# Layer 0 of a four-layer graph network: adjacency tiles transposed by the DMA engines, codes made in place, a fifth accumulator

## The chip, the core and the metric

The kernel runs on one core of a Trainium2 chip. A core has five engines that run side by side, each with its own queue of instructions: TensorE (PE, matmuls and transposes; PEld is its loading of weights), VectorE (DVE), ScalarE (ACT), GpSimd (POOL) and SyncE (SP, which here only issues DMAs). Sixteen DMA engines move data between HBM and the on-chip memory SBUF. TensorE writes its results to PSUM, a memory of eight banks.

The metric is the device time of one launch in microseconds (us). The trace comes from a separate execution with the hardware profiler on; its own time stands beside its span in the table below.

## The reference

Four graph layers follow each other on a node matrix x (4096 x 256, float32) and one adjacency matrix adj (4096 x 4096, int32, about 0.8% ones). Each layer adds its result to x. Layer 0 is the one that the change touches, and of it the attention:

```python
h = relu(layernorm(x))
Wh = h @ W
e = Wh @ a_src + (Wh @ a_dst).T
e = where(e > 0, e, 0.2 * e)
e = where(adj > 0, e, -9e15)
h_attn = softmax(e, axis=1) @ Wh
...   # dense branches on Wh, gating with h_attn, layernorm; x = x + result
```

Layer 1 averages neighbours (adj == 1), layer 2 is a second attention of the same kind (slope 0.01), layer 3 a dot-product attention masked by adj. All of them need adj with its columns on the partitions, that is transposed, since the matmul `acc += y.T @ v` sums over the columns of adj.

## The kernel before

**Codes.** An adjacency tile of 128 rows x 1024 columns is a unit. There are 128 units: g runs over 8 blocks b of 512 rows, 4 quarters q of the columns and 4 row tiles r in a block. Units are turned once, in layer 0, and changed into two-valued bf16 codes (a very large number where adj is 0, a very small one where it is 1): ACT computes exp(scale * adj + bias) with scale and bias of fixed logarithms. Four units (r = 0 to 3) fill one tile `turned[b, q]` (128 x 4 x 8 x 128 bf16, 1 MB). SP stores every such tile to HBM (`codesT`, L368), from where layers 1, 2 and 3 load it.

**How a unit is turned (`fresh(g)`, L345 to L361).** POOL issues the load, which also casts int32 to bf16 (L351, eight buffers `adj_t`). PE makes eight 128x128 transposes with the bf16 identity `identb` into one PSUM bank `cT` (L354, a pool with a single buffer, L343). ACT reads that bank and writes the codes to SBUF (L358).

**Preparation.** `block0(b)` (L378), for eight row blocks staggered by two ticks: three units made fresh, the load of x (L382, on SP), layernorm on DVE, POOL and ACT (L133), transposes, projection with W (L201 to L214), and then `reach`, below.

**Attention (`run`, L271).** A block has 16 pairs of column tiles, 128 pairs in all. Iteration n of the loop does, in program order: `ahead(n)`, which makes unit n + 24 fresh (`UPB` = 16, `FRESH` = 8) and at every fourth n issues the store; `reach(n + 19)`, two DVE steps (L229) of a running minimum over the columns, from which the next block's row maxima come; `logits`, two DVE instructions (L265) and one on POOL that subtracts the codes (L269); and for the pair three iterations earlier (`lag`) two exponentials on ACT (L295) and eight matmuls (L306, each issued as two 128x257 passes) into four accumulators, one for each row tile. At the end of a block, reciprocals of the sums (L314) and `finish0`, which scales the accumulators into `xs` by turns on ACT (L336) and DVE (L334).

**The maxima.** At a block's last `reach`, `run` is copied by ACT (L235), transposed by PE (L238), reduced by DVE, transposed again (L248), copied (L250), and sent through HBM by two small DMAs on SP (L251, L253). The result `ab_row` is needed by L263 (ACT), after which DVE can begin the logits of the next block.

**Order.** The program is written in one order, and a planner reorders the instructions of each engine by dependencies and its own estimate of their times; so the trace shows L265 and L229 in turn although each comes twice in a row in the program. What it decided is then fixed: each engine, SP among them, goes through its queue in order and waits at the first instruction that isn't ready. Buffers are pools with a number of slots; an instruction that needs a slot waits for the last reader of its previous tile.

**PSUM.** Eight banks: `run`, `top`, `b` one each, `cT` one, and four accumulators. Layer 2 runs the same class with five accumulators (L794), loading stored codes instead of making them.

## Time and profile before

| | |
|---|---|
| median of 3 runs | 3092.0 us (3091.15 to 3102.12) |
| the profiled execution | 3085.67 us, span 3083.9 us |
| layer 0's preparation | 0 to about 112 us |
| layer 0's attention | about 112 to 630 us |
| its blocks end (first L314 of each) | 178.9, 247.2, 313.7, 381.2, 447.3, 514.6, 573.1, 629.7 us |
| PE busy over the span | 2869.8 us, 93% |
| DVE, ACT, POOL busy | 1851.4, 1271.7, 873.3 us |
| L354, transposes of adjacency | 1024, 83.2 us busy on PE |
| L358, codes on ACT | 128, 141.5 us busy |
| L351, loads | 128 of 256 KB, 4.5 us from issue to landing |
| L368, stores of codes | 32 of 1 MB, 5.1 us |

Times in the trace count from the span's start. A row of a group of instructions gives the line, the engine, the operation, output and inputs, the number of instructions and their mean duration; PE's durations overlap, as matmuls are pipelined, so what one costs is read from the pitch between starts. A window's row gives start and end, length, then the busy time of PE, PEld, DVE, ACT and POOL with the number of instructions, the share of the clock that TensorE was granted, the mean busy share of the sixteen DMA engines and GB/s. The waits name an instruction, what ended its wait, the sum, the count and the longest. An arrow <- stands before what released an engine.

### The profile page before, as it was taken

The numbers are of one execution on the slowest core, as the hardware profiler recorded it, in microseconds if no ns is written. First come the engines' busy times: TensorE is split into PE (matmuls) and PEld (weight loads), VectorE is DVE, ScalarE is ACT, GpSimd is POOL, SyncE is SP. The second block draws the span as 40 slices with busy tenths as digits, with TensorE's granted clock in tenths as the row PEclk, the third lists the DMA queues.
The fourth block names the chain that finished last, engine by engine and source line by source line (L and its number), as shares of the span: only waits on it lengthen the run. The fifth ranks groups of instructions, "written<-read, shape, count | busy, mean of one in ns | idle before, by whom it ended". The sixth has DMA issues, their size and how long they took to land.

```text
span 3083.9 us, 34813 instructions
## 1 busy us (share of the span) xinstructions
PE 2869.8 (93%) x13344; PEld 2336.0 (76%) x13344; DVE 1851.4 (60%) x3306; ACT 1271.7 (41%) x1924; POOL 873.3 (28%) x605
## 2 busy tenths in 40 slices
PE   5799999979999999699977999999999999999999
PEld 4688888845555555588856888788888888888888
DVE  5767676324444444544479888755856656656653
ACT  5655655358888884400044443444211211211211
POOL 3556665532333233100016555661000000000000
PEclk9899999989999999899998999999999999999999
DMA  8666664054444341234322222202111111111100
GB/s 209 144 132 136 126 139 110 7 178 129 142 129 132 122 132 40 87 110 147 99 103 82 76 77 81 76 7 69 57 38 37 58 37 37 58 37 37 56 8 7
DMA packets 103127, 268.75 MB, mean 87 GB/s; under 512 B 10704, under 2 KB 24272, under 8 KB 94768
## 3 DMA queue, kind: packets, MB, share of 16 engines
q1 hardware_dynamic: 79104, 220.30, 21.4%
q0 software_dynamic: 22464, 45.51, 8.7%
q8 instruction: 104, 1.70, 0.2%
q10 hardware_dynamic: 1392, 0.72, 0.1%
q14 instruction: 63, 0.52, 0.1%
HBM read 262.22 MB, written 37.81 MB: 97 GB/s over the span
## 4 chain that ended last, share of the span: by engine, by line
PE 27%; issue 25%; DVE 3%; POOL 2%; DMA 1%; ACT 1%; POOLq 0%; DVEq 0%; ACTq 0%
PE acc L306 12%; PE acc L723 8%; PE s L150 3%; PE mm L150 2%; PE acc L960 2%; DVE run L229 1%; POOL y L269 1%; DMA turned<-codesT 1%; DVE y L265 1%; POOL pl_rs L116 1%; POOL out_dram L973 1%; DVE pl_st L121 0%; ACT y L295 0%; DVE hT L109 0%; PE tp L144 0%
## 5 line engine op out<-in xcount | busy, mean ns | idle before, releaser
L306 PE MATMUL acc<-v,y 128*128 128x257 f32 x4096 | 927.1, 385 | 42.5 <-ACT y L295 19.9
L306 PEld LDWEIGHTS acc<-v,y 128*128 128x128 f32 x4096 | 774.4, 192 | 158.1 <-ACT hp L754 22.7
L269 POOL TENSOR_TENSOR y<-y,turned 128x1024 f32<-128x1024 f32 x256 | 547.1, 2150 | 307.7 <-DVE y L265 267.5
L295 ACT ACTIVATE y<-y,sdst 128x512 f32<-128x512 f32 x512 | 342.9, 714 | 367.7 <-POOL y L269 367.5
L265 DVE SCALAR_TENSOR_TENSOR y<-ab_row,cdst,b 128x512 f32<-128x512 f32 x512 | 362.1, 743 | 180.2 <-PE acc L306 115.8
L960 PE MATMUL acc<-v,y 128*128 128x257 f32 x2048 | 454.5, 380 | 0.4 <-DVE rden L968 0.4
L150 PE MATMUL s<-qT,hT 128*128 128x256 f32 x2048 | 445.2, 379 | 0.7 <-ACT qT L908 0.7
L150 PEld LDWEIGHTS s<-qT,hT 128*128 128x128 f32 x2048 | 389.0, 190 | 54.2 <-ACT qT L908 1.4
L960 PEld LDWEIGHTS acc<-v,y 128*128 128x128 f32 x2048 | 387.1, 190 | 55.9 <-issue 0.8
L953 ACT ACTIVATE y<-y 128x1024 f32<-128x1024 f32 x128 | 132.2, 1055 | 714.3 <-DVE y L952 710.0
L229 DVE SCALAR_TENSOR_TENSOR run<-turned,sd,run 128x512 f32<-128x512 bf16 x496 | 373.4, 753 | 49.8 <-DMA turned<-codesT 28.3
L513 ACT ACTIVATE sign<-a,limits 128x1024 bf16<-128x1024 int32 x256 | 293.8, 1148 | 79.6 <-DMA a<-in_adj_dram 75.0
L973 POOL DMA_DIRECT2D out_dram<-o x32 | 17.4, 543 | 933.7 <-DVE rden L968 931.1
L723 PE MATMUL acc<-v,eq 128*128 128x512 f32 x1024 | 239.3, 395 | 0.1
L922 DVE SCALAR_TENSOR_TENSOR y<-code,s 128x512 f32<-128x512 bf16 x256 | 175.8, 687 | 100.5 <-PE s L150 100.2
L723 PEld LDWEIGHTS acc<-v,eq 128*128 128x128 f32 x1024 | 192.6, 188 | 44.9 <-DVE eq L719 0.3
L952 DVE TENSOR_TENSOR y<-y,top 128x1024 f32<-128x1024 f32 x128 | 146.2, 1216 | 43.0 <-PE top L946 43.0
L929 DVE TENSOR_TENSOR mx<-mx,y 128x512 f32<-128x512 f32 x224 | 154.8, 691 | 7.4
L358 ACT ACTIVATE turned<-cT,log_wide 128x1024 bf16<-128x1024 bf16 x128 | 141.5, 1106 | 33.5 <-PE cT L354 33.2
L719 DVE TENSOR_SCALAR eq<-code 128x4096 fp32r<-128x4096 bf16 x32 | 73.4, 2293 | 114.8 <-PE acc L723 114.8
L150 PE MATMUL mm<-hsT,w_L_gnn_W_hz 128*128 128x512 f32 x256 | 117.4, 598 | 0.6 <-DVE hsT L576 0.6
L354 PE MATMUL cT<-identb,adj_t 128*128 128x128 bf16 x1024 | 83.2, 226 | 36.4 <-DVE identb L67 18.5
(222 smaller groups left out, 2717.3 us busy)
## 6 DMA issues: line engine op xcount, KB each, us to landing
a<-in_adj_dram SPq DMA_DIRECT2D x128, 512.0 KB, 3.8
adj_t<-in_adj_dram POOLq DMA_DIRECT2D x128, 256.0 KB, 4.5
codesT<-turned SPq DMA_DIRECT2D x32, 1024.0 KB, 5.1
code<-codesT SPq DMA_DIRECT2D x128, 256.0 KB, 3.8
turned<-codesT SPq DMA_DIRECT2D x32, 1024.0 KB, 5.4
code<-codesT SPq DMA_DIRECT2D x64, 512.0 KB, 4.9
ab_row<-l_ab_d SPq DMA_DIRECT2D x16, 512.0 KB, 3.9
xs<-in_x_dram SPq DMA_DIRECT2D x8, 512.0 KB, 11.0
```

Source lines behind the costliest of these rows:

```text
L150: nc.tensor.matmul(out=ps, lhsT=lhsT_of(k), rhs=rhs_of(k), start=(k == 0), stop=(k == n - 1))
L229: nc.vector.scalar_tensor_tensor(st["run"], code, self.sd[:, j, 1:2], st["run"], ALU.subtract, ALU.min)
L265: nc.vector.scalar_tensor_tensor(y[:, :, k, :], st["ab"][:, 0, :, :], self.cdst[:, c + k : c + k + 1], st["b"], ALU.add, ALU.max,)
L269: nc.gpsimd.tensor_tensor(y, y, mask[:, :, c % QT : c % QT + 2, :], ALU.subtract)
L295: nc.scalar.activation(y[:, :, k, :], y[:, :, k, :], AF.Exp, bias=self.sdst[:, c + k : c + k + 1],)
L306: nc.tensor.matmul(out=accs[b][r], lhsT=y[:, r, k, :], rhs=self.v[:, c + k, :], start=(c + k == 0), stop=(c + k == NT - 1),)
L513: nc.scalar.activation(sign, a, AF.Sign, bias=limits[:, v : v + 1], accum_out=over[:, t, v, q : q + 1],)
L723: nc.tensor.matmul(out=acc, lhsT=eq[:, ts(c, P)], rhs=v1[:, c, :, :], start=(c == 0), stop=(c == NT - 1),)
L922: nc.vector.scalar_tensor_tensor(y[:, :, c : c + 2, :], st["code"][:, :, c : c + 2, :], -BIG / UNIT, ps, ALU.mult, ALU.add,)
L929: nc.vector.tensor_tensor(mx, mx, y[:, :, c : c + 2, :], ALU.max)
L952: nc.vector.tensor_tensor(part, part, top, ALU.subtract)
L960: nc.tensor.matmul(out=accs[r], lhsT=st["y"][:, r, c, :], rhs=v3[:, c, :], start=(c == 0), stop=(c == NT - 1),)
```

## The change

A unit is no longer transposed by PE. `fresh` is split in three steps that run at different leads. `load(g)` issues the load on POOL as before. `turn(g)` issues on SP one transposing DMA from the loaded tile to its quarter of `turned[b, q]`, SBUF to SBUF. ACT then computes the codes in place in `turned`. When unit g is made fresh, the load of unit g + 6 and the transposing DMA of unit g + 3 are issued just before its exponential; the first call issues six loads and three transposes ahead. The numbers of buffers stay at eight each. The identity in bf16 and the PSUM pool `cT` go, and the free bank becomes a fifth accumulator of layer 0's attention. Layers 1 to 3 and the dense part of layer 0 are as they were.

```diff
-    identb = const.tile([P, P], BF16, name="identb")
-    nc.vector.tensor_copy(identb, ident)
...
+    LOADED, TURNED = 6, 3
...
-            ps_c = es.enter_context(tc.tile_pool(name="ps_c", bufs=1, space=PSUM))
-
-            def fresh(g):
-
+            raw, units = {}, NRB * UPB
+
+            def load(g):
                 b, q, r = g // UPB, g % UPB // RB, g % RB
-                t = b * RB + r
-
-                a = adj_p.tile([P, QW], BF16, tag="adj", name="adj_t")
-                nc.gpsimd.dma_start(out=a, in_=adj[ts(t, P), ts(q, QW)])
-                ps = ps_c.tile([P, QW], BF16, tag="cT", name="cT")
-                for i in range(QT):
-                    nc.tensor.transpose(ps[:, ts(i, P)], a[:, ts(i, P)], identb)
+                raw[g] = adj_p.tile([P, QW], BF16, tag="adj", name="adj_t")
+                nc.gpsimd.dma_start(out=raw[g], in_=adj[ts(b * RB + r, P), ts(q, QW)])
+
+            def turn(g):
+                b, q, r = g // UPB, g % UPB // RB, g % RB
                 if r == 0:
                     turned[b, q] = turned_p.tile([P, RB, QT, P], BF16, tag="turned", name="turned")
-                ct = turned[b, q][:, r, :, :]
+                nc.sync.dma_start_transpose(turned[b, q][:, r, :, :], raw.pop(g))
+
+            def fresh(g):
+
+                if g == 0:
+                    for k in range(LOADED):
+                        load(k)
+                    for k in range(TURNED):
+                        turn(k)
+                if g + LOADED < units:
+                    load(g + LOADED)
+                if g + TURNED < units:
+                    turn(g + TURNED)
+                b, q, r = g // UPB, g % UPB // RB, g % RB
+                ct = turned[b, q][:, r, :, :].rearrange("p c i -> p (c i)")
                 nc.scalar.activation(
-                    ct.rearrange("p c i -> p (c i)"), ps, AF.Exp,
-                    scale=math.log(UNIT / WIDE), bias=log_wide,
+                    ct, ct, AF.Exp, scale=math.log(UNIT / WIDE), bias=log_wide
                 )
...
-            att.run(es, LEAD, 4, ahead)
+            att.run(es, LEAD, 5, ahead)
```

## The prediction, made before the changed kernel ran

> **What bounds the kernel now.** I read the page's busy shares first, then cut layer 0 by the reciprocals that close each block of rows (L314 starts at 178.89, 247.15, 313.66, 381.19, 447.31, 514.58, 573.15 and 629.75 us) and asked for the windows between them. The first matmul of the attention is at 114.9 us, so layer 0's attention runs from about 112 to 629.75: 517.7 us of 3083.9. All that the change touches lies there and in the 112 us ahead of it.
>
> Windows of the span, columns window, length, then busy us of PE, PEld, DVE, ACT, POOL, clock, DMA share, GB/s. The first two are preparation, the next three are blocks 0, 3 and 7 of layer 0's attention, the last two are blocks of layer 2's:
>
> ```profile
> 50.00:60.00 10.00, 8.40 (x65) 7.20 (x65) 5.79 (x16) 10.00 (x19) 3.19 (x5) 1.00 1.02 222
> 60.00:70.00 10.00, 9.45 (x81) 8.22 (x80) 7.16 (x21) 9.89 (x20) 2.54 (x5) 1.00 0.97 211
> ...
> 112.00:178.89 66.89, 62.49 (x336) 53.73 (x337) 50.98 (x81) 40.12 (x56) 51.06 (x32) 0.95 0.39 82
> 313.66:381.19 67.53, 64.79 (x390) 55.57 (x389) 46.39 (x76) 39.43 (x54) 42.63 (x33) 1.00 0.63 133
> 573.15:629.75 56.60, 55.78 (x257) 48.50 (x256) 14.01 (x25) 14.36 (x23) 20.71 (x10) 1.00 0.00 1
> ...
> 1813.32:1875.08 61.76, 58.24 (x261) 50.00 (x261) 49.14 (x78) 25.03 (x39) 34.86 (x17) 0.97 0.22 77
> 1996.69:2052.76 56.07, 54.89 (x254) 47.65 (x255) 32.73 (x53) 24.50 (x38) 33.55 (x17) 1.00 0.03 10
> ```
>
> The attention is bound by TensorE: 64.8 of 67.5 us, while DVE has 46.4, POOL 42.6, ACT 39.4. Block 7, which has no adjacency left to turn, takes 56.6. The preparation from 40 to 80 us is bound by ACT (10.0 of 10 us) with the DMA engines full beside it (share 1.02). The timeline inside block 3 shows what a pair costs on PE:
>
> ```profile
> 331.60 0.61 PE L354 MATMUL cT<-identb,adj_t 128*128 128x128 bf16 x8
> 332.05 3.69 PE L306 MATMUL acc<-v,y 128*128 128x257 f32 x16
> 335.57 0.61 PE L354 MATMUL cT<-identb,adj_t 128*128 128x128 bf16 x8
> 336.02 3.69 PE L306 MATMUL acc<-v,y 128*128 128x257 f32 x16
> ```
>
> A pair begins every 3.97 us (335.57 - 331.60). In block 7 the DVE's y (which waits for PE there) comes every 3.47 us (582.57, 586.04, 589.51), so eight transposes cost PE 0.50 us. The windows of L354 count 128 of them in each of blocks 1 to 5, 80 in block 0, 40 in block 6, none in block 7; 264 lie ahead of 112 us.
>
> ```profile
> q1 hardware_dynamic: 79104, 220.30, 21.4%
> q0 software_dynamic: 22464, 45.51, 8.7%
> ...
> adj_t<-in_adj_dram POOLq DMA_DIRECT2D x128, 256.0 KB, 4.5
> codesT<-turned SPq DMA_DIRECT2D x32, 1024.0 KB, 5.1
> ```
>
> These lines of the page price a unit (one 128x1024 adjacency tile) on the DMA engines. Between 80 and 112 us units came every 2.21 us (POOL issued at 97.51, 99.72, 101.94) at a share of about 1.04: 2.3 us of all sixteen engines for one load and a quarter of a store.
>
> **What the Trainium skill says.** (1) "Advanced Engine Details and Errata", X-Bar Transpose (TRN2): transposing DMAs are as fast as plain ones, 350 to 400 GB/s. (2) "DMA: Bandwidth & Descriptors", Latency and other measured facts: 261 GB/s effective with a non-contiguous middle dimension. A unit is 262,144 bytes, so these give estimates of 0.7 and 1.0 us. (3) "VectorE: DVE Perf Modes", The three transpose paths: 1309 ns for 128x128 by the crossbar; eight in series would be an estimate of 10.5 us a unit. (4) The DMA page again, Issuing engines are not separate DMA queues: SP's and POOL's DMAs share the same sixteen engines; the shares above 1 in the preparation agree. The trace of before holds no transposing DMA, so (1) to (3) can't be checked in it.
>
> **The change part by part.**
> 1. PE transposes in the attention go: 760, or 95 units, x 0.50 us = 47.5 us off the engine that bounds it. Gone too are PE's waits for the one PSUM tile cT: gaps before L354 of 0.95 to 1.5 us, one or two a block.
> 2. Fifth accumulator. At block ends PE waits about 1.1 us for ACT to empty the first accumulators (gaps at 249.4, 315.9, 383.4, 449.6). Layer 2's attention, the same code with five, takes 56.07 for a block without turning, layer 0's block 7 takes 56.60: 0.5 us a block.
> 3. What is late next. A floor for a block: 16 x 3.47 = 55.5, PE's transposes for the maxima 1.4 (L238 4 x 0.286, L248 0.27), the boundary 0.5, PE's wait for DVE's ab 0.9 (gaps before L248): 58.3. DVE's busy 46.4 a block plus its wait for b (7.93 us once a block, at 364.73) makes 54.3, close below. Layer 2's blocks that prepare the next one take 59.1 to 61.8 (one 65.5) with a heavier finish and waits for loads that layer 0 has not. I take 59.5.
>    Block 0: 66.9 - 10 x 0.50 - 1.3 of gaps = 60.6. Blocks 1 to 5: 297.5. Block 6: 58.57 - 5 x 0.50 = 56.1. Block 7: 56.1. Sum 470.3 against 517.7: 47.4 us gained. With 58.3 the gain is 53, with 61.3 it is 38.
> 4. ACT's exponentials now read SBUF: L358 1106 ns from PSUM; the nearest row with SBUF as source, L953 (128x1024), 1055. 128 of either, taken as equal. ACT keeps its order, and one that waits for a transfer holds up the exps, copies and L133 behind it.
> 5. SP gains 128 issues. A plain one takes 0.32 us there; no row shows a transposing one, so between that and T, and as long as it stays below a pair's 3.47 SP keeps up. Each waits for its load (issued three units before, 12 us; landing 4.5) and for a turned buffer, whose last reader is POOL's L269 some two pairs back, which POOL passes about eight pairs before PE. Behind it on SP stand codesT stores, for which nobody in layer 0 waits, and L251 and L253, for which ACT L263 and then DVE wait: in block 3 L263 starts at 364.06, its first exps could be done 5.4 us later, PE needs them at 382, so 12 us of delay are covered. After that each us costs one, once a block.
> 6. POOL's loads waited for PE cT (71.4 us from 130 to 540); they now wait for the transposing transfer that frees one of eight buffers, five pairs back. Behind them stands L269, with 42.6 of 67 us used; covered unless a transfer takes over 15 us.
> 7. DMA engines: 2.3 us + T a unit, against a pace of 59.5 / 16 = 3.72. T lies between 0.7 and 10.5; I take 1.0, since two pages speak of rates and the third of one small transfer, where latency weighs most. Then 3.3 us, 89%: hidden in the attention.
> 8. In the preparation it is not hidden. Up to its last code it must turn 27 units (27 us more), loads only 30 units where before had some 37 by 97 us (about 11 us less) and stores two groups fewer (about 5 less): 11 us more for the engines. From 30 to 50 us they idle (shares 0.39 and 0.67): 9 us. The cover is thus nearly used up; stalls of ACT's queue cost more, PE's wait of 1.5 us before abT at 94.8 goes. I take +6 us, between -2 and +20.
> 9. identb and its copy (0.19 us of DVE): nothing.
>
> Sum: -47.4 + 6 = -41 us. The profiled execution took 3085.67 (span 3083.9), which becomes about 3044; the median of the runs shown, 3092.0, lies 6.3 above it, so 3051 for the median. Layers 1 to 3 are untouched.
>
> **The rivals.**
> A. As above, but DVE or the chain through ab_row sets 61.3 a block and the preparation loses 20 us: -38 + 20 = -18, 3074. For it: layer 2's blocks. Against: its finish and load waits are absent.
> B. The DMA engines saturate: with T = 2.0 a unit needs 4.3 us, above today's 67.1 / 16 = 4.19; the attention gains nothing (+5) and the preparation loses 27 more (+33 in all), less a few: about 3122. For it: shares of 1.02 to 1.06. Against: 261 GB/s or more.
> C. The slower side, one mechanism: the transposing transfer itself is paced, on SP or at the crossbar, at T a unit, one after another. Layer 0's attention then ends near 13 (first load) + 128 T + 85 (the last 24 pairs at 3.5). That equals today's 630 at T = 4.2, the point from which it decides. T = 5 gives 738, +108: 3200; 10.5 gives 1442, +812: 3904. For it: 1309 ns for one block of 128x128. Against: the rates.
>
> **How the numbers follow.** Forecast 0.58, A 0.10, B 0.12, C 0.20. What a measurement of this kernel can tell from no change is about 0.5%, 15.5 us. Faster: 0.55 of the forecast and 0.07 of A, 0.62. Same: 0.03 of each of the forecast, A and B, 0.09. Slower: 0.09 of B and all of C, 0.29. The likeliest case's own range is 3034 to 3074; with A, B and the mild part of C the range is 3030 to 3200, which leaves out most of C (0.14) and little below.
>
> **What would show it.** Right: layer 0's full blocks at 58 to 61 us, PE about 95% busy with L306 pitched 3.47 a pair; the first L306 at 113 to 135 us; DMA share 0.8 to 1.0 in the attention; transposes landing within 3 to 6 us. B shows shares at 1.0 and ACT's code exps waiting for the DMA with blocks of 66 or more. C shows SP or the queue issuing one transfer every 4 us or more, PE idle, and DVE L229 waiting for codes. Wrong altogether: if the planner puts L251 or L253 behind a transfer that waits, L263 is over 12 us late in each block.

## The result, and the profile after

The changed kernel takes 3244.95 us (median of 4 runs, 3223.08 to 3263.71) against 3092.51 us (median of 4 runs of the kernel before on the same chip): a ratio of 1.0483, 95% interval 1.0413 to 1.0554. The forecast was 3051, its range 3030 to 3200. The profiled execution took 3249.88 us, its span is 3248.1 us, 164.2 us more than before.

I cut layer 0 as in the prediction, by the first matmul of the attention and the first reciprocal at the end of each block (L312 in the changed kernel's numbering, which is two lines less than before up to the codes; the codes are now L370, their store L379, the load L349, the transposing DMA L355).

| us | first matmul | block 0 | 1 | 2 | 3 | 4 | 5 | 6 | 7 |
|---|---|---|---|---|---|---|---|---|---|
| before | 114.9 | 64.0 | 68.3 | 66.5 | 67.5 | 66.1 | 67.3 | 58.6 | 56.6 |
| after | 191.8 | 78.9 | 82.7 | 77.4 | 80.7 | 82.1 | 69.4 | 62.1 | 56.6 |

Layer 0's attention ends at 781.6 instead of 629.7 us: 151.9 us later, 76.9 of them lost in the preparation and 75.0 in the attention. The other 12 us are spread behind it, and their cause is open.

The page of the changed kernel, its busy shares, slices, queues, groups and DMA issues (columns as in the prediction's lines; a slice is 81 us):

```profile
PE   1367777898899999969996899999999999999999
...
DMA  9979888703434444223432222210211111111100
...
q1 hardware_dynamic: 214272, 253.87, 28.2%
q0 software_dynamic: 22464, 45.51, 8.5%
...
L370 ACT ACTIVATE turned<-turned,log_wide 128x1024 bf16<-128x1024 bf16 x128 | 143.7, 1143 | 77.4 <-DMA turned<-adj_t 76.9
...
L349 POOL DMA_DIRECT2D adj_t<-in_adj_dram x128 | 70.6, 554 | 260.9 <-DMA turned<-adj_t 243.3
...
adj_t<-in_adj_dram POOLq DMA_DIRECT2D x128, 256.0 KB, 6.9
```

PE stands at 1 to 8 tenths in the first eight slices, where the DMA engines stand at 7 to 9. The queue that SP feeds has 135,168 packets more than before (79,104). 131,072 of them are the change: 1024 packets of 256 bytes for each of the 128 units. A load lands after 6.9 us instead of 4.5, and both the codes on ACT and the loads on POOL now wait for transposing DMAs (76.9 and 243.3 us).

Windows of the changed kernel (start and end, length, busy us of PE, PEld, DVE, ACT, POOL, clock, DMA share, GB/s): three of the preparation, block 2 of the attention whole, then that block's middle and its end, and block 7:

```profile
40.00:60.00 20.00, 4.77 (x12) 3.57 (x12) 4.04 (x20) 2.31 (x3) 2.48 (x6) 0.79 1.30 104
60.00:80.00 20.00, 6.77 (x24) 4.83 (x24) 4.37 (x12) 6.85 (x12) 2.91 (x5) 0.67 1.31 109
100.00:120.00 20.00, 4.61 (x14) 3.39 (x13) 1.68 (x5) 2.10 (x5) 4.79 (x8) 0.59 1.24 171
353.40:430.80 77.40, 59.97 (x261) 50.82 (x261) 49.14 (x80) 40.85 (x54) 41.81 (x33) 0.90 0.86 170
358.40:420.00 61.60, 54.01 (x236) 46.26 (x237) 35.40 (x54) 31.70 (x41) 29.20 (x25) 0.92 1.02 202
420.00:430.80 10.80, 5.96 (x27) 4.55 (x25) 9.21 (x14) 5.06 (x8) 7.63 (x4) 0.98 0.01 3
725.00:781.60 56.60, 55.78 (x257) 48.49 (x257) 14.00 (x24) 14.43 (x23) 20.76 (x10) 1.00 0.00 1
```

In these windows of the preparation no compute engine is busy for more than 7 of 20 us; ACT, which was full there before, has 2.1 to 6.9. The DMA engines' share is 1.24 to 1.31, yet they move only 104 to 171 GB/s, less than the 211 to 222 of before.

One queue has no pause there, SP's. It goes from one transposing DMA straight to the next, and none of them waits for a load or for a slot in the preparation. The first line is the changed kernel's, the second that of e5 below, which leaves the loads out:

```profile
23.41 102.21 SPq L355 DMA_TRANSPOSE turned<-adj_t  x28
...
23.84 43.28 SPq L359 DMA_TRANSPOSE turned<-adj_t  x28
```

Beside the loads a transposing DMA thus keeps SP for 3.65 us, without them for 1.55, and the codes can come no faster. The loads wait in turn for the buffers that these transfers free, and on POOL the layernorm's L114 stands behind the loads. Its last comes at 138.8 us; only then does ACT catch up, and abT follows at 179.0 instead of 94.8.

In the attention PE does as much useful work as forecast (block 7, with nothing to turn, is 56.60 us as before), but a block that turns units has two parts: some 62 us with the DMA engines full (1.02), then 11 us in which they do nothing at all (0.01).

The timeline of PE in that block shows where PE's 17 us of idle time lie (start, length, instructions, and in brackets the idle time before them and its cause):

```profile
359.04 32.57 PE L304 MATMUL acc<-v,y 128*128 128x257 f32 x142 [10.27 <-ACT xs L335]
...
402.90 0.37 PE L246 MATMUL abT<-ident,ab 128*8 128x128 f32 x1 [6.95 <-DVE ab L244]
403.07 22.19 PE L304 MATMUL acc<-v,y 128*128 128x257 f32 x94
```

There are two gaps, 6.95 us ahead of abT and 10.27 us at the block's start. Before, the matmuls waited 0.6 us ahead of abT (1.1 in block 0) and 0.4 to 0.8 at the block's start; in its block 3:

```profile
316.98 2.87 PE L306 MATMUL acc<-v,y 128*128 128x257 f32 x12 [0.68 <-ACT xs L336]
...
356.95 0.27 PE L248 MATMUL abT<-ident,ab 128*8 128x128 f32 x1 [0.64 <-DVE ab L246]
```

The waits between 200 and 600 us (sum, count, longest) lead from PE back to the DMA:

```profile
POOL adj_t L349 <- DMA turned<-adj_t: 119.4, 44, 11.2
...
ACT turned L370 <- DMA turned<-adj_t: 59.7, 36, 4.8
DVE run L227 <- ACT turned L370: 57.4, 9, 10.6
...
PE acc L304 <- ACT xs L335: 40.7, 5, 13.0
...
PE abT L246 <- DVE ab L244: 34.4, 5, 8.6
```

Read from below: abT waits for the maxima, the last step of the running minimum (L227) waits for a code (10.6 us at the longest), the code (L370) for its transposing DMA. abT stands in PE's queue ahead of matmuls that could run, so PE stops. The second gap hangs on what follows: from abT to the copy of `ab_row` (L261) the changed kernel needs 14.7 to 21.1 us in blocks 0 to 4, the kernel before 5.7 to 7.4. In block 2 these are 18.0 us (in brackets the share in block 3 of before, of 7.1). 5.4 pass before ACT, which has codes ahead of it that wait for transposing DMAs, copies abT (0.3); 6.1 lie between the issues of the small store and of the load, with a store of codes between them on SP (1.3); 6.2 lie between the load's issue and the copy of `ab_row` (5.2). Then the next block's first exponentials run on ACT, and L335, which frees PE's accumulators, stands behind them.

How much time the DMA engines spend I read from the trace by adding up the durations of all packets of a stretch, divided by 16 engines, in us (a load has all of POOL's packets):

| stretch | length | per load | per transposing DMA | stores and rest | sum |
|---|---|---|---|---|---|
| before, preparation | 114.9 | 1.67 (41 units) | | 37.7 | 106.0 |
| after, preparation | 191.8 | 2.04 (40) | 2.81 (32) | 42.3 | 213.8 |
| before, block 3 | 67.5 | 1.91 (16) | | 12.0 | 42.5 |
| after, block 2 | 77.4 | 1.69 (16) | 1.71 (16) | 12.1 | 66.6 |

Packets of one engine overlap, so that such a sum can exceed the length by up to a third; it is an upper bound of the work in it. In the preparation it doubles; in a block it rises by 24 us, and with the 10.8 us in which no packet runs it gives the block's 77.4: while packets run, the mean share is about 1. Half of the 256-byte packets last 18 ns with loads beside them and without. What grows is a tail: between 40 and 120 us 11% of them last over 100 ns and make 57% of their sum, in e5 0.3% and 8%. Whether such a packet works or waits the trace doesn't say.

### The profile page after: what moved, and what is told of

Same layout as the page of the kernel before. It is cut to its first block, busy times and chain, and to the rows that moved or that the text cites. A ratio compares the mean times of both kernels' runs of the same rounds, so it can differ in the third digit from the quotient of the medians.

```text
span 3248.1 us, 33118 instructions
## 1 busy us (share of the span) xinstructions
PE 2859.5 (88%) x12320; PEld 2310.3 (71%) x12320; DVE 1857.9 (57%) x3305; ACT 1278.2 (39%) x1924; POOL 872.4 (27%) x605
## 4 chain that ended last, share of the span: by engine, by line
PE 25%; issue 24%; DVE 3%; POOL 2%; DMA 1%; ACT 1%; POOLq 0%; DVEq 0%; ACTq 0%; SPq 0%
PE acc L304 12%; PE acc L734 7%; PE s L148 3%; PE acc L971 2%; PE mm L148 2%; DVE run L227 1%; POOL y L267 1%; DVE y L263 1%; POOL pl_rs L114 1%; POOL out_dram L984 0%; DMA turned<-codesT 0%; DVE pl_st L119 0%; ACT h L131 0%; DVE hT L107 0%; ACT y L293 0%
## 5 line engine op out<-in xcount | busy, mean ns | idle before, releaser
L304 PE MATMUL acc<-v,y 128*128 128x257 f32 x4096 | 943.5, 393 | 102.1 <-ACT xs L335 46.1
L304 PEld LDWEIGHTS acc<-v,y 128*128 128x128 f32 x4096 | 801.9, 197 | 236.5 <-ACT xs L335 50.0
L267 POOL TENSOR_TENSOR y<-y,turned 128x1024 f32<-128x1024 f32 x256 | 546.2, 2152 | 353.8 <-DVE y L263 314.0
L971 PE MATMUL acc<-v,y 128*128 128x257 f32 x2048 | 454.5, 380 | 0.4 <-DVE rden L979 0.4
L227 DVE SCALAR_TENSOR_TENSOR run<-turned,sd,run 128x512 f32<-128x512 bf16 x496 | 373.2, 752 | 103.4 <-ACT turned L370 66.7
L971 PEld LDWEIGHTS acc<-v,y 128*128 128x128 f32 x2048 | 387.1, 190 | 55.9 <-issue 0.8
L964 ACT ACTIVATE y<-y 128x1024 f32<-128x1024 f32 x128 | 132.2, 1055 | 714.3 <-DVE y L963 710.0
L524 ACT ACTIVATE sign<-a,limits 128x1024 bf16<-128x1024 int32 x256 | 293.8, 1148 | 82.7 <-DMA a<-in_adj_dram 78.2
L370 ACT ACTIVATE turned<-turned,log_wide 128x1024 bf16<-128x1024 bf16 x128 | 143.7, 1143 | 77.4 <-DMA turned<-adj_t 76.9
L148 PE MATMUL mm<-w,hT 128*128 128x258 f32 x256 | 71.6, 436 | 85.5 <-ACT v L207 53.4
L349 POOL DMA_DIRECT2D adj_t<-in_adj_dram x128 | 70.6, 554 | 260.9 <-DMA turned<-adj_t 243.3
L730 DVE TENSOR_SCALAR eq<-code 128x4096 fp32r<-128x4096 bf16 x32 | 73.3, 2292 | 114.9 <-PE acc L734 114.9
```

What stands on the lines that cost most here:

```text
L148: nc.tensor.matmul(out=ps, lhsT=lhsT_of(k), rhs=rhs_of(k), start=(k == 0), stop=(k == n - 1))
L227: nc.vector.scalar_tensor_tensor(st["run"], code, self.sd[:, j, 1:2], st["run"], ALU.subtract, ALU.min)
L267: nc.gpsimd.tensor_tensor(y, y, mask[:, :, c % QT : c % QT + 2, :], ALU.subtract)
L304: nc.tensor.matmul(out=accs[b][r], lhsT=y[:, r, k, :], rhs=self.v[:, c + k, :], start=(c + k == 0), stop=(c + k == NT - 1),)
L524: nc.scalar.activation(sign, a, AF.Sign, bias=limits[:, v : v + 1], accum_out=over[:, t, v, q : q + 1],)
L971: nc.tensor.matmul(out=accs[r], lhsT=st["y"][:, r, c, :], rhs=v3[:, c, :], start=(c == 0), stop=(c == NT - 1),)
```

## The experiments

The theories at the start: **D**, the DMA engines, on which loads and transposing DMAs meet, pace layer 0; and **Q**, POOL's queue, in which loads that wait for a transposing DMA stand ahead of other work (in the preparation the layernorm's L114, which came every 21 to 33 us between loads). Some expectations name further theories by a letter and say in words what they are. Each kernel was compared with the kernel before on the same chip. In the table, times are medians of 2 to 18 runs (two in e6, e9 and e10); first matmul and blocks are from the profiled execution.

| run | us | ratio, 95% interval | first matmul | blocks 0 to 6 |
|---|---|---|---|---|
| e1 | 3239.7 | 1.0469 [1.0436, 1.0503] | 188.2 | 72.6 84.4 75.8 80.9 81.2 71.3 64.3 |
| e2 | 3242.0 | 1.0481 [1.0455, 1.0506] | 189.1 | 76.4 82.0 75.7 79.4 80.9 69.7 63.3 |
| e3 | 3198.0 | 1.0335 [1.0304, 1.0365] | 139.5 | 78.8 81.1 76.0 80.3 80.7 71.8 63.3 |
| e4 | 3147.6 | 1.0185 [1.0155, 1.0216] | 160.9 | 66.2 66.9 67.1 67.3 66.1 66.9 58.6 |
| e5 | 3089.6 | 0.9984 [0.9974, 0.9995] | 117.6 | 62.4 64.2 63.7 66.5 65.2 64.9 61.7 |
| e6 | 3229.7 | 1.0427 [1.0394, 1.0459] | 189.2 | 82.4 81.1 76.7 78.1 79.6 64.4 61.4 |
| e7 | 3216.8 | 1.0401 [1.0342, 1.046] | 179.8 | 78.2 77.9 76.2 78.5 78.9 62.6 60.8 |
| e8 | 3259.3 | 1.0517 [1.0476, 1.0559] | 180.1 | 83.0 84.5 80.6 87.0 82.1 74.5 58.8 |
| e9 | 3227.5 | 1.043 [1.0403, 1.0457] | 223.6 | 102.5 64.0 63.8 66.4 63.5 64.4 62.9 |
| e10 | 3120.8 | 1.0085 [1.0059, 1.0111] | 125.4 | 68.6 66.1 65.6 72.6 71.0 69.1 61.0 |
| e11 | 3098.4 | 1.001 [0.9999, 1.0021] | 117.3 | 63.1 65.4 64.6 65.1 68.2 65.6 63.6 |
| e12 | 3205.5 | 1.0357 [1.0331, 1.0383] | 190.3 | 95.2 68.1 67.2 67.7 67.2 67.0 58.6 |
| f1 | 3240.5 | 1.0466 [1.0439, 1.0493] | 184.5 | 82.8 81.3 76.1 80.8 87.4 64.9 61.7 |
| f2 | 3243.0 | 1.0471 [1.0452, 1.0491] | 173.8 | 73.3 85.4 75.7 80.5 82.0 71.8 59.2 |
| f3 | 3125.6 | 1.0098 [1.0082, 1.0115] | 128.4 | 66.2 70.2 72.6 70.2 70.3 71.3 58.1 |
| f4 | 3192.2 | 1.0308 [1.0287, 1.033] | 142.4 | 75.2 83.1 76.7 78.6 80.9 66.2 63.2 |
| g1 | 3164.7 | 1.0229 [1.0212, 1.0246] | 151.7 | 72.2 72.7 73.6 72.5 73.1 65.8 58.9 |
| g2 | 3230.0 | 1.0435 [1.042, 1.0451] | 146.1 | 80.9 88.5 87.2 89.8 85.8 64.1 62.4 |

### One part at a time: e1 to e4

e1 takes layer 0's L114 off POOL: the power is computed by ACT as a logarithm and an exponential.

```diff
...
-        rs = rstd_of(small, mv, BT, "pl")
...
+            nc.scalar.activation(rs, mv[:, :, 1], AF.Ln, bias=eps_c)
+            nc.scalar.activation(rs, rs, AF.Exp, scale=-0.5)
```

> The changed kernel with one thing moved: in layer 0's preparation the layernorm's power (v + eps) ** -0.5 is made by ACT (Ln, then Exp) instead of POOL. Theory Q (POOL's queue: L114 stands behind loads that wait for a transposing transfer, and the layernorm waits for L114): the first attention matmul, at 190 us in the changed kernel, comes at 120 to 140, and the time falls by 50 to 70 us to about 3180. Rival D (loads and transposes share the DMA engines, 3.9 us a unit, and that alone paces the preparation): the first matmul stays at 170 or later and the time within 20 us of 3245.

The first matmul moved only from 191.8 to 188.2 us, but this doesn't clear Q. The preparation's own work ended 17.5 us earlier, with abT at 161.5 in place of 179.0. Then the small store of the maxima, issued at 162.2, took 15.6 us to land, as the wait of the load behind it shows:

```profile
SPq L258 <- DMA l_ab_d<-abT_sb: 15.6, 1, 15.6
```

From 153 us on SP had issued seven stores of codes of 1 MB, and the engines moved 359 GB/s while the small one waited. So L114's place behind the loads is worth up to 17 us of the preparation, which e1 lost again on the way of the maxima. The larger part is not Q's: in e1 too the first 28 transposing DMAs follow each other on SP, 3.94 us each.

e2 is the changed kernel with four accumulators.

```diff
-            att.run(es, LEAD, 5, ahead)
+            att.run(es, LEAD, 4, ahead)
```

> The changed kernel with four accumulators in layer 0, as before. If the fifth bank is worth what layer 2's blocks suggested (0.5 us a block), the time is 3245 to 3250. Rival: the fifth accumulator let the planner place finish0 behind the next block's exponentials (ACT L335 released PE 46 us in all), then four accumulators give back up to 40 us: 3205 to 3230.

3242.0 against 3245.0: the fifth accumulator does nothing that can be measured while the codes are late.

e3 and e4 split the change by time. In e3 PE turns units 0 to 23 as before and the DMA the rest; in e4 the DMA turns units 0 to 23 and PE the rest, with four accumulators.

```diff
+            FIRST, LAST = 24, units     # e3;  e4: 0, 24
...
             def fresh(g):
-                if g == 0:
+                if not FIRST <= g < LAST:
+                    by_pe(g)
+                    return
+                if g == FIRST:
```

> Units 0 to 23 turned by PE as before (the bank for it is free again in the attention), the rest by transposing DMAs, five accumulators. If preparation and attention lose independently (the changed kernel: about 75 us each), the first attention matmul is at about 115 us, the blocks stay at 77 to 83 us, and the time is about 3170. Rival: the attention's loss is an after-effect of the late preparation, then the blocks fall to about 60 us and the time to 3060.

> The reverse: units 0 to 23 by transposing DMAs, the rest by PE, four accumulators. Independent losses: first matmul at about 190 us, blocks of 66 to 68 us, 3170. Rival (all of the loss sits in the attention's queues and the preparation only shifts it): blocks shorter than 66 and a time near 3100.

e3 gives back 52 of the preparation's 77 us (139.5), and its blocks are those of the changed kernel; e4 keeps the blocks of the kernel before and loses in the preparation (160.9). Against the kernel before, e3 costs 3.35%, e4 1.85%, and the whole change 4.83%: the two losses are separate and nearly add up. There isn't one late start that runs through the layer.

### What the DMA engines carry: e5, e9, e10, e11, e12

e5 leaves out the adjacency loads of units 8 to 127 (the first eight tiles are turned again and again) and keeps everything else; e11 is the same with four accumulators. e10 instead loads 16 of a unit's 1024 columns for those units, into the tile that was turned eight units before, so that all waits and as many packets are there, but few bytes. e9 loads them whole, into five spare tiles that nobody reads, so that the bytes are there and no load waits for a transposing DMA.

```diff
             def load(g):
                 b, q, r = g // UPB, g % UPB // RB, g % RB
...
+                if g >= 8:
+                    raw[g] = kept[g % 8]
+                    # e10: dma_start(out=raw[g][:, 0:16], in_=adj[ts(b * RB + r, P), q * QW : q * QW + 16])
+                    # e9:  dma_start(out=spare, in_=adj[ts(b * RB + r, P), ts(q, QW)])
+                    return
```

> The changed kernel with the adjacency loads of units 8 to 127 left out: the eight tiles loaded first are turned again and again, so everything else, the 128 transposing DMAs among it, is as in the changed kernel. Theory D (a transposing DMA is slow only beside load packets: 1.4 us a unit in the attention's bursts, 3.7 to 3.9 in the preparation): the pace of the first 24 units falls to 1.3 to 1.8 us, the first attention matmul comes at 115 to 130 us, and the time falls by 60 us or more. Rival S (SP or the crossbar paces it, whatever else moves): pace above 3 us, first matmul after 170. For the attention: if its loss is queue order behind codes that wait for a turned buffer, blocks stay at 74 to 82 us; if it is the loads too, they fall to about 60.

> The reverse: each load from unit 8 on fetches 16 of its 1024 columns into the tile that was turned eight units before, so POOL's waits for the transposing DMAs are those of the changed kernel while the bytes of the loads are almost gone. Theory D: about as the run without loads, pace 1.4 to 1.8, first matmul 115 to 130, blocks 62 to 67, 3085 to 3110. Rival Q: first matmul at 150 or later or blocks above 72, 3170 or more.

> As the run without loads, but loads 8 to 127 are issued at their places into five spare tiles that nobody reads; the transposing DMAs turn the eight tiles loaded first. So the DMA traffic of the changed kernel is back, while no load on POOL waits for a transposing DMA. Theory D (packets of loads and of transposing DMAs hinder each other on the DMA engines): pace of the first 24 units 3 us or more, first matmul at 160 or later, time 3200 to 3250. Rival Q (POOL's queue: loads that wait for a transfer hold up the layernorm and L267): pace below 2.8, first matmul below 140, blocks 62 to 67, time 3090 to 3120.

> The run without loads (3089.6 us, blocks 62 to 66) with four accumulators. What the fifth bank is worth when codes are not late: by my 0.5 us a block, 3093 to 3095; if the planner's place for finish0 makes it a loss, below 3085.

The same two windows of the preparation, in e5:

```profile
40.00:60.00 20.00, 15.01 (x59) 11.36 (x60) 10.22 (x28) 16.75 (x28) 2.02 (x3) 1.00 1.01 190
60.00:80.00 20.00, 15.34 (x65) 10.84 (x64) 12.14 (x33) 18.23 (x34) 1.01 (x1) 0.91 1.08 235
```

and in e10:

```profile
40.00:60.00 20.00, 11.35 (x42) 8.86 (x42) 10.39 (x38) 11.11 (x19) 9.29 (x16) 1.00 1.21 186
60.00:80.00 20.00, 13.11 (x49) 8.97 (x48) 8.88 (x25) 14.32 (x27) 8.75 (x15) 0.83 1.17 233
```

Without loads ACT has its 17 to 18 us of 20 back and the preparation is as fast as before the change (117.6 against 114.9), with all 32 transposing DMAs in it. With the waits but few bytes it is 125.4. With both, 191.8. So the waits alone cost some 8 us, and the bytes of the loads beside the transposing DMAs the other 66. SP shows it directly: it needs 45.0 us for the first 28 transposing DMAs in e10, 43.3 in e5 and 102.2 in the changed kernel. The packet sums change too: a transposing DMA takes 1.49 us of all engines in e5, 1.51 in e10, and 2.81 in the changed kernel. Its packets of 256 bytes last 46 ns in the mean between 40 and 120 us there, and 23 in e5; the loads' packets last 249 ns against 206 in the kernel before.

In the attention e5 has blocks of 62.4 to 66.5 us, e10 of 65.6 to 72.6, the changed kernel of 77 to 83. Both waits and bytes take part. e11 against e5 is the fifth accumulator where no load is in the way. They ran on two chips; as shares of the kernel before, 1.0010 against 0.9984, it is worth some 8 us, with intervals that just don't touch.

e9 did not do what it was made for. As nobody reads the spare tiles, nothing held its loads back: 103 units' worth of load packets had run before the first matmul, and none ran after 300 us. Its first matmul at 223.6 shows what that many loads cost, and its blocks of 64 us are those of e5. It says nothing on the attention. It warns against the packet sums, though: beside those loads a transposing DMA took only 1.60 us of all engines, but between 70 and 175 us 72 loads passed and fewer than 10 transposing DMAs, and single ones kept SP for 10 to 17.6 us. What such a transfer costs its queue is not in the sum of its packets.

e12 is the kernel before with 120 transposing DMAs of a fixed tile into tiles that nobody reads.

```diff
...
+                if g >= 8:
+                    idle = idle_p.tile([P, QT, P], BF16, tag="idle", name="idle")
+                    nc.sync.dma_start_transpose(idle, kept[0])
```

> The kernel before, PE still turning every unit, plus 120 transposing DMAs on SP of one fixed tile into tiles that nobody reads, one for each unit from 8 on, issued after its load. Nothing waits for them but SP's own queue and what shares the DMA engines. Theory D: the loads slow down beside them (their 2 KB packets above 206 ns on average between 40 and 105 us, landings above 4.5 us), the preparation grows by 30 us or more, time 3130 or more. Rival: no cost but queueing on SP, 3092 to 3105.

The first matmul came at 190.3, as in the changed kernel, but for another reason. The timeline of e12's SP queue:

```profile
100.53 24.69 SPq L365 DMA_TRANSPOSE idle<-kept  x4
...
177.17 0.53 SPq L251 DMA_DIRECT2D l_ab_d<-abT_sb  x1
```

The small store of the maxima (L251), ready since 98 us, stood behind thirty-three transposing DMAs. From 126 us on, when no load runs, each takes SP about 1.65 us; the four ahead of that took 24.7. With the queue clear of them, from block 2 on, its blocks were those of the kernel before. So e12's time shows the price of transposing DMAs ahead of a small urgent one in SP's queue.

Its preparation also shows the contention that it was made for. The loads' packets last 245 ns between 40 and 105 us, where the kernel before has 206, and from 56.7 to 89.3 us three transposing DMAs took SP 10.1 to 11.4 us each. Still abT came at 96.3 us against 94.8: here no code waits for them.

### Buffers and queues: e6, e7, e8, f1, f2, f4, g2

e6 has fourteen `adj_t` buffers and loads twelve units ahead, f1 fourteen buffers and loads six ahead, e7 nine `turned` tiles.

```diff
...
-    LOADED, TURNED = 6, 3
+    LOADED, TURNED = 12, 3          # e6; f1 keeps 6
...
-            adj_p = es.enter_context(tc.tile_pool(name="adj", bufs=8))
+            adj_p = es.enter_context(tc.tile_pool(name="adj", bufs=14))     # e6 and f1
-            turned_p = es.enter_context(tc.tile_pool(name="turned", bufs=8))
+            turned_p = es.enter_context(tc.tile_pool(name="turned", bufs=9))     # e7 alone
```

> The changed kernel with 14 buffers for loaded tiles instead of 8 and loads 12 units ahead. Theory D (DMA engines): more buffers move no faster, pace of the first 24 units 3.5 us or more, first matmul at 180 to 195, time within 20 us of 3245. Rival L (the preparation is a loop of eight buffers, load landing, transfer, release, and latency paces it): pace below 2.6 us, first matmul below 150, 3200 or less.

> The changed kernel with nine turned tiles instead of eight. Theory W (in the attention the codes come late because each group of four transposing DMAs waits on SP for POOL L267 to release a turned tile; 146.9 us of such waits): with one more tile the group starts four pairs earlier, blocks 1 to 4 fall from 77 to 83 us to 65 to 72, the time to about 3190. Rival P (the planner fills the new slack with more work ahead, and the in-order queues meet the late codes just as before): blocks stay above 75, time within 20 us of 3245.

> The changed kernel with fourteen adj_t buffers in place of eight, loads still issued six units ahead. A load then takes the buffer of a unit whose transposing DMA was issued eleven units before instead of five, so POOL should hardly wait for a transposing DMA any more (119 us between 200 and 600 us in the changed kernel). Theory W (the attention's 75 us come from POOL's queue: loads that wait stand ahead of L267): blocks 0 to 5 fall from 77-83 us to 66-70, first matmul stays near 188, time about 3180. Theory S (they come from SP's queue, where the small DMAs L249 and L251 stand behind transposing DMAs and stores that wait) and theory D (the packets' mutual slowing in the attention): blocks stay at 75 to 83, time 3230 to 3250.

None opened the blocks: blocks 0 to 4 take 77 to 82 us in e6, 76 to 79 in e7, 76 to 87 in f1. Nor is a loop of eight buffers what paces the preparation: with fourteen the first matmul comes at 189.2 (e6) and 184.5 (f1). f1 was to take POOL's wait away and didn't:

```profile
POOL adj_t L349 <- DMA turned<-adj_t: 115.0, 45, 11.2
```

119.4 us had become 115.0: with more buffers POOL's loads ran further ahead, 10 to 13 units ahead of the transposing DMAs instead of 4 to 7, and met the same wait there. W was not tested by it. e7 has the largest gain, 28 us, some 12 of it in the preparation; its interval overlaps that of the changed kernel.

In layer 0, e8 copies abT on DVE and issues the stores of the codes on ACT's queue; f2 issues the two small DMAs of the maxima on ACT's queue; f4 joins e3, f1 and f2.

```diff
...
-            nc.scalar.copy(abT, ps)
+                nc.vector.tensor_copy(abT, ps)                              # e8
...
-                    nc.sync.dma_start(out=codesT[b][q], in_=turned[b, q])
+                    nc.scalar.dma_start(out=codesT[b][q], in_=turned[b, q]) # e8
...
-            nc.sync.dma_start(out=self.ab_d[b].rearrange("v r i -> (v r) i"), in_=abT)
+            ab_q = nc.scalar if self.tag == "l0" else nc.sync                         # f2, f4
+            ab_q.dma_start(out=self.ab_d[b].rearrange("v r i -> (v r) i"), in_=abT)   # f2, f4
```

> The changed kernel with two steps of layer 0's maxima chain taken out from behind the codes: the copy of abT (L248) goes from ACT, where it stood behind code exponentials that wait for transfers, to DVE; and the stores of codes go from SP to ACT's queue, so that SP's ab_row load no longer stands behind a store that waits for an exponential. Theory C (the chain from abT to ab_row, 18 us against 7 before, starves the next block): blocks 1 to 4 fall by 6 to 12 us, time 3195 to 3220. Rival: the other end of the chain (DVE's own order, L239 behind L227 that waits for codes) sets it, then blocks move by less than 4 us.

> The changed kernel with layer 0's two small DMAs of the maxima (L249, L251) issued from ACT's queue instead of SP's; all else as it is. Theory S (SP's queue): the chain from abT to L261 falls from 18 us to about 8, full blocks from 77-83 us to 68-73, time about 3190. Theories W and D: the chain is shorter but the blocks lose it elsewhere, since the codes for the next maxima come no earlier: blocks 75 to 82, time 3225 to 3255.

> The first 24 units by PE as in e3, the rest by the transposing DMA; fourteen adj_t buffers with loads six units ahead; L249 and L251 on ACT's queue; five accumulators. If queues cause the attention's loss (W, S or both): first matmul near 139, blocks 63 to 68, time 3090 to 3130. If the packets do (D): first matmul near 139, blocks 75 to 80 as in e3, time 3185 to 3205.

e8 is a miss (blocks of 81 to 87). In f2 the way from abT to the copy of `ab_row` stayed at 13.3 to 19.9 us although SP's queue was out of it, so SP's queue is not the only reason. Its block 3 has 18.8 us. 8.3 pass before the store goes out at 468.32, since on ACT's queue it stands behind codes that wait for transposing DMAs; 2.4 lie between the store and the load; and `ab_row` is there at 478.78, 8.1 us after the load's issue, where the kernel before has about 5. So f2 traded one queue's order for another's, and a part of the delay lies behind the issue. f4 has e3's time (3192.2 against 3198.0, intervals that overlap).

g2 takes up the end of the block, where the DMA engines stand still. The SP timeline of the changed kernel there:

```profile
408.59 0.28 SPq L249 DMA_DIRECT2D l_ab_d<-abT_sb  x1
411.75 0.35 SPq L379 DMA_DIRECT2D codesT<-turned  x1
414.67 0.32 SPq L251 DMA_DIRECT2D ab_row<-l_ab_d  x1
431.60 18.77 SPq L355 DMA_TRANSPOSE turned<-adj_t  x8
```

Nothing is issued for 17 us; SP's longest wait is of 17.5 us, for L267 to free a slot of `turned`. L267 waits there for the next block's first logits, these for `ab_row`, and that for the last codes. It is a ring: codes, maxima, logits, slot, transposing DMA, codes. g2 is e3 with five tiles of their own for the transposing DMAs, from which ACT makes the codes, so that SP doesn't wait for a slot.

```diff
...
-                nc.sync.dma_start_transpose(turned[b, q][:, r, :, :], raw.pop(g))
+                flat[g] = flat_p.tile([P, QT, P], BF16, tag="flat", name="flat")
+                nc.sync.dma_start_transpose(flat[g], raw.pop(g))
```

> As e3 (first 24 units by PE, the rest by transposing DMA, five accumulators), but the transposing DMA writes into one of five tiles of its own, and ACT computes the codes from there into turned. SP then no longer waits for L267 to free a slot of turned (147 us in the changed kernel). Theory B (those slots stop the DMA engines at the end of each block, where their share is 0.01 for 11 us): the share at the end of a block is above 0.3, blocks 64 to 70, time 3090 to 3140. Theory D: blocks stay at 75 to 80 as in e3, time 3185 to 3205.

Blocks of 81 to 90 us, worse than e3. The waits of g2's SP queue between 200 and 560 us show that the ring only closed in another place, at ACT, which now holds the slots and waits in its turn:

```profile
SPq L357 <- ACT turned L393: 135.6, 28, 13.7
SPq L357 <- ACT y L295: 115.8, 20, 22.9
```

### Both kinds of packets in the attention, and fewer of them: g1, f3

g1 is the kernel before, PE turning every unit; each unit from 24 on also has its loaded tile turned by a DMA into a tile that nobody reads. Here the two kinds of packets must meet in the attention, and no code waits for a transposing DMA.

```diff
...
+                if g >= 24:
+                    idle = idle_p.tile([P, QT, P], BF16, tag="idle", name="idle")
+                    nc.sync.dma_start_transpose(idle, a)
                 ps = ps_c.tile([P, QW], BF16, tag="cT", name="cT")
```

> The kernel before (PE turns every unit, four accumulators), to which each unit from 24 on adds a transposing DMA of its own loaded tile into a tile that nobody reads; twelve adj_t buffers. The transposing DMA can't start before its load, so both kinds of packets now meet in the attention itself, while no code waits for a transposing DMA. Theory D (the packets' mutual slowing alone sets the attention): loads come late, blocks 0 to 5 of 75 us or more, DMA share near 1, time 3140 or more. Theory B (the loss comes from the late codes and the waits that hang on them, slots of turned among them): blocks 67 to 70 as in the kernel before, share 0.75 to 0.95, time 3090 to 3115.

Windows of g1, its block 3 whole and ten us of it; then DVE's waits for the maxima, five times each, in g1 (200 to 560 us) and in the kernel before (200 to 500 us):

```profile
370.30:442.80 72.50, 66.28 (x390) 56.75 (x390) 46.48 (x75) 39.47 (x54) 42.77 (x33) 0.98 0.99 182
380.00:390.00 10.00, 10.00 (x59) 8.71 (x59) 5.78 (x10) 7.00 (x9) 7.63 (x7) 1.00 1.14 153
...
DVE y L265 <- ACT b L263: 65.8, 5, 14.1
...
DVE y L265 <- ACT b L263: 37.6, 5, 8.3
```

Blocks 1 to 4 take 72.5 to 73.6 us, between the two expectations, at a mean share of 0.99 to 1.03. By packet sums a load takes 1.79, a transposing DMA 1.98, the stores and the rest 0.83 us a unit, 4.6 in all. That looks as if the DMA engines set the pace, but the lost 6 us lie elsewhere. In the first 40 us of block 3 PE has no gap, at shares up to 1.14. What grew is the way of the maxima: from abT to the copy of `ab_row` it takes 11.5 to 13.2 us instead of 5.7 to 7.4, 3 to 5 of them before SP issues the small store (0.6 before). DVE's wait at its end is 5.6 us longer a block. So the transposing DMAs that nobody reads cost the block what they cost the small urgent DMAs, on SP's queue and behind it. That full engines alone lengthen a block is not shown.

f3 turns only every fourth unit of the attention by DMA (26 units), loaded four and turned two units ahead; the rest goes through PE.

```diff
...
+                k = g + 2
+                if k >= FIRST and k % STEP == FIRST % STEP and k < units:
+                    turn(k)
+                if g < FIRST or g % STEP != FIRST % STEP:
+                    by_pe(g)
+                    return
```

> The kernel before with only every fourth unit of the attention (25 of the units from 27 on) transposed by the DMA, loaded four and transposed two units ahead; the others and the preparation by PE, four accumulators. Theory D in its strong form (each transposing DMA beside loads costs 1.5 to 2 us of all engines more than its sum): 4 units of 16 a block leave the DMA engines at about 2.7 us a unit against a pace of 4.2, so nothing is lost and PE saves 4 x 0.5 = 2 us a block: blocks 64 to 66, time 3075 to 3090. Theories W and S: waits of POOL or SP at each such unit still cost a part: blocks 68 to 72, time 3100 to 3130.

3125.6, with full blocks of 70 to 73 us. The DMA engines had room (a share of 0.71 in block 2), so it isn't D in its strong form; from abT to the copy of `ab_row` it took 9.1 to 9.9 us in place of 5.7 to 7.4. Even four transposing DMAs a block cost more than the 2 us of PE that they save.

No version was found that beats the kernel before. e5 equals it and leaves the loads out.

## Why the prediction was wrong

**The step that failed is the seventh, "2.3 us + T a unit … T lies between 0.7 and 10.5; I take 1.0 … Then 3.3 us, 89%: hidden in the attention", and the eighth, which uses the same T for the preparation.** The two pages' rates were taken for what a transposing DMA costs beside loads, and the time that it holds its queue was left out of the preparation. Measured:

- T, 1.0 in the text. By packet sums it is 1.49 us without loads (e5); in the attention 1.71 in the changed kernel and 1.98 in g1; in the preparation 2.81. The Trainium skill's "Advanced Engine Details and Errata", X-Bar Transpose (TRN2), has transposing DMAs as fast as plain ones at 350 to 400 GB/s, and "DMA: Bandwidth & Descriptors", Latency and other measured facts, 261 GB/s with a non-contiguous middle dimension. In e5, with no load beside them, they follow each other every 1.38 us, and 262,144 bytes in that time are 190 GB/s. The measurement decides.
- The 2.3 us of a load and a quarter of a store were read in a stretch of the preparation. The window of block 3 that the prediction shows holds the attention's own figure: 0.63 x 67.53 / 16 = 2.66 us.
- In the preparation the text has 27 us more for turning, 11 less for loads and 5 less for stores, all of it spread over sixteen engines. Measured by packets, turning takes 90.0 more (32 units at 2.81), the loads 13.2 more and the rest 4.6 more: 107.8 us instead of 11. And it is not spread: the first 28 transposing DMAs hold SP one after another for 102.2 us. That sets the pace of the codes, and the preparation lost 77 us instead of 6. e5, with 43.3 us for the same 28, has the preparation of before.
- In the attention the sum is 2.45 + 1.71 = 4.16 us in the changed kernel (66.6 / 16) and 4.6 in g1, above the 3.72 that the text wanted to stay under. The cover that it counted on isn't there. But g1 shows that such a sum is not yet the pace of a block. The loss that the traces show runs through late codes and the way of the maxima: 6.95 and 10.27 us of idle PE in block 2.

Rival B had the resource and even the price, T = 2.0 and 4.3 us a unit, at a chance of 0.12. It gave 3122, since it let the DMA engines work through every block without a pause and priced the preparation at the same T. What it lacks is the ring, with 10 to 14 us a block in which no packet runs (blocks 1 to 4), and the preparation's price.

Rival C is half right, and the range had left out most of it. What it said would show it is there in the preparation: SP issues 20 transposing DMAs in 80 us between 40 and 120 us, one every 4.0 us, and PE is idle. Its reason, a pace of the transfer's own, is not: without loads they pass every 1.38 us. Its 3200 for T = 5 stood as the upper end of the range, and the measured time lies above it.

By the other steps:

1. PE's transposes went, and block 7's length is what it was. But e5, which has all of the change except the loads and the waits for them, has a mean of 64.5 us over blocks 0 to 5 against 66.6 before: 2.1 us a block and not the 7 of step 3.
2. The fifth accumulator: 0.5 us a block in the text; some 8 us in all where codes are early (e11 against e5), nothing where they are late (e2).
3. "A floor for a block … 58.3 … I take 59.5" was too low by 5 us even without loads. In e5 PE still waits 27.4 us at six block starts between 200 and 600 us, where the text has 0.5 for each, and the way from abT to `ab_row` takes 9.8 to 12.4 us, up to 4.5 of it before ACT copies abT. The 0.9 and 1.1 us that the text read as PE's waits are too high; its matmuls waited 0.6 and 0.7.
4. ACT's exponentials: 1143 ns against the 1055 to 1106 of the text. 37 ns x 128 are 5 us of an engine with room. Right.
5. "as long as it stays below a pair's 3.47 SP keeps up": the median of 1.34 us stays below, but the preparation's 3.65 doesn't. The 12 us of delay that are "covered" were used up in the attention: the way of the maxima takes 8 to 15 us longer, and the codes came late as well. The text's last sentence ("wrong altogether") describes this closely. Of block 2's 11 us more, about 5 pass on ACT ahead of the copy, about 5 between the two small DMAs on SP, and 1 behind the load's issue.
6. POOL's loads waited 119.4 us in 400. Whether L267 behind them suffered could not be separated: f1 left the wait as it was. e10, which keeps the loads that wait but few of their bytes, has a mean of 68.8 us over blocks 0 to 5, against 64.5 in e5 and 78.5 in the changed kernel: about a third of the difference.
9. `identb`: nothing, as said.

The shares above 1 in the preparation, which the text read as two queues on the same engines, show only that packets overlap. That loads and transposing DMAs hinder each other is shown by the loads' packets, 249 ns instead of 206, and by SP's 3.65 us instead of 1.55.

Open is why a transposing DMA holds SP for so long beside loads, and how a block's loss divides between bytes and waits. That the packets of the two kinds hinder each other at the engines would fit the numbers, but how they do is only argued. No run kept the preparation's loads and transposing DMAs apart in time.

## What to carry to other kernels

Before moving work from an engine to the DMA engines, write their time for one unit of the loop from the window of that very loop (share x length / units), add the new transfer at a price measured beside such traffic, and compare the sum with the pace wanted. Do the same for the queue that issues it: here a transposing DMA held SP for 1.55 us or 3.65, depending on what ran beside it, and a rate from a page gave neither. Then look at the small urgent transfers of the loop. Here they slowed down first, and the ring that runs through them (codes, maxima, logits, slot) turned the shortage into idle time of everything. A full DMA share is not yet the reason: g1 had it, and its loss lay on the way of the maxima. A test transfer that nobody reads must be tied to the data of its stage, or it runs far ahead and tests another stage.

## What the runs showed of the hardware

- A transposing DMA of 128x1024 bf16 within SBUF is 1024 packets of 256 bytes. Where no load runs, SP takes 1.33 us for one (median) and they follow each other every 1.38 us (e5). Beside the preparation's loads SP took 3.65 us for one in the changed kernel, and 10 to 17.6 us for single ones in e9.
- The mean busy share of the DMA engines reached 1.31 while they moved 104 to 109 GB/s: here a full share went with a low rate. With the loads left out the same stretch moved 190 to 235 GB/s at 1.01 to 1.08.
- By packet sums the cost of a transposing DMA depends on what runs beside it: 1.49 us without loads, 1.60 to 2.81 beside them.
- The small store of the maxima, issued behind seven stores of 1 MB, took 15.6 us to land (e1).
